# The first expert mixture's outputs: stored in slot order and gathered by token, in place of scattered to token order

## The chip, the core and the metric

The kernel runs on one core of a Trainium2 chip. Five engines work side by side, each on its own queue of instructions in a fixed order: TensorE (PE; its weight loads are listed as PEld), VectorE (DVE), ScalarE (ACT), GpSimd (POOL) and SyncE (SP). They wait for each other through semaphores, and every transfer between the chip's memory and the core's own memory (SBUF) is issued by one of the queues and moved by 16 shared DMA engines. The metric is the device time of one execution in microseconds (us); the median over the runs is compared.

## The reference

The input is 8 sequences of 256 tokens with 256 channels. It goes through three sublayers, each on a layer-normalised copy and added back:

```
x = x + 0.5 * ffn(layernorm(x))
x = x + attn(layernorm(x))
x = x + 0.5 * ffn(layernorm(x))
```

`ffn` is a mixture of 8 experts. Each of the 2048 tokens takes the two experts with the highest gate value; each expert computes `(silu(x @ w_gate) * (x @ w_up)) @ w_down` with a hidden width of 176. The two results are weighted by their gate probabilities and added to a shared feed-forward part of hidden width 352. `attn` has 16 heads of width 128 with one key and one value head; an index score picks the 32 best earlier keys of every query, and the softmax runs over those.

## The kernel before, in words

The 2048 tokens are 16 tiles of 128 (NT = 16), and `x` stays in SBUF all the time. The three sublayers follow one another: `ffn(0, ...)`, the attention, `ffn(1, ...)`. The order on every engine is fixed when the program is built; the building framework moves independent instructions past each other, so that work of one stage can stand among the next one's.

In `ffn`, `layernorm` normalises the tiles and also stores them to `xn_dram` in the chip's memory (line 249). `route` works out, for each token and each of its two choices, a slot: the slots of one expert are consecutive and start at a multiple of 128, so that the slots fall into blocks of 128 rows with one expert each. 37 blocks always run (ND), two more only when they are needed (`rare`, NB = 39). From the slots `route` derives, for each row of each block, the token to fetch (`token`) and the row to write (`dest`).

For block b, `fetch` (L488) has POOL gather 128 rows of `xn_dram` by `token` with an indirect DMA. PE transposes them (`turn`, `px`, L499), multiplies them by the expert's gate and up weights (`widen`, `pgu`, L511), transposes the hidden values (`turn_hidden`, `ph`, L539) and multiplies by the down weights (`narrow`, `py`, L547). ACT makes `sl` (L521) and copies `py` to `y` (L555), DVE makes `h` and `hT` (L523, L541). Then POOL scatters the block's rows with a second indirect DMA (L557) to `y_dram`, each row to the place of its token and choice. Fetches run up to six blocks ahead (XB = 6), and there are four `y` buffers. SP meanwhile loads attention weights, one load per block (L118). The shared part of some tiles (`shared`, L451, L470, L477, L480) is left for after the blocks.

`combine` (L597) brings the expert results of one token tile back. For the first mixture it is called in the attention's `begin`, before the layer norm of the tile:

```python
parts = y_dram[NT * P : (K + 1) * NT * P, :].rearrange("(k i p) d -> i p k d", k=K, p=P)
yg = pool.tile([P, K, D], F32, tag="yg", name=f"yg_{n}_{i}", bufs=bufs)
nc.sync.dma_start(out=yg, in_=parts[i])
```

So it is one plain load of 256 KB by SP (L599), and then two DVE instructions on `x` (L601), weighted with `wt`. There are three `yg` buffers here. In the built order all 16 loads stand on SP right behind the last weight load, and the 32 DVE instructions stand between the shared parts, the layer norms and the first index scores of the attention.

The attention's first steps are `select_keys(0)` and four times `index_queries` and `add_heads`: PE makes `pqi` (L637) and `pi` (L698), ACT copies `qi` (L644) and makes `r` (L706), DVE adds to `index` (L711, L713). POOL zeroes the first 32 columns of each `qi` buffer before (L632). Later POOL scales the softmax weights (L779) and stores them by plain DMAs of its own (L790).

Of the kernel before, what the change touches and what calls it, by code (L numbers as in the profile page):

```python
# [8 lines left out]
F32 = mybir.dt.float32  # L9
BF16 = mybir.dt.bfloat16  # L10
I32 = mybir.dt.int32
# [4 lines left out]
P = 128  # L16
# [7 lines left out]
def macaron_kernel(  # L24
# [19 lines left out]
    nc = tc.nc  # L44

    B, S, D = x_in.shape
    NT = B * S // P
# [8 lines left out]
    K = 2  # L56
# [5 lines left out]
    NB = (NT * P * K) // P + E - 1  # L62
    ND = (NT * P * K) // P + E // 2 + 1
# [14 lines left out]
    small = ctx.enter_context(tc.tile_pool(name="small", bufs=3))  # L78
    psum = ctx.enter_context(tc.tile_pool(name="psum", bufs=2, space=bass.MemoryType.PSUM))
    dram = ctx.enter_context(tc.tile_pool(name="dram", bufs=1, space=bass.MemoryType.DRAM))  # L80


    x = res.tile([P, NT, D], F32, name="x")
# [16 lines left out]
    for g in groups:  # L100
# [6 lines left out]
        out=wsd_sb[:, 0:nfull, :],  # L107
        in_=sw_down[0 : nfull * P, :].rearrange("(c p) d -> p c d", p=P),
# [40 lines left out]
    for h0 in range(0, H, HL):  # L149
        for k in range(KD):  # L150
            cols = slice(h0 * HD, (h0 + HL) * HD)
# [8 lines left out]
    for t, val in ((cap, 3e38), (cbias, 0.0)):  # L160
        nc.gpsimd.memset(t, val)
        nc.gpsimd.affine_select(
            out=t,
            in_=t,
# [10 lines left out]
        out=before,  # L175
        in_=before,
# [9 lines left out]
    def counted(name, pattern, base=0, channel=0, dtype=F32, pool=const):  # L186
        t = pool.tile([P] + [n for _, n in pattern], dtype, name=name, bufs=1)
        nc.gpsimd.iota(
            t, pattern, base=base, channel_multiplier=channel,
            allow_small_or_imprecise_dtypes=True,  # L190
        )
        return t
# [62 lines left out]
    def route(n, lg, place, block, pool, keep, meanwhile):  # L255
# [5 lines left out]
        def t(name, shape, dtype=F32):  # L261
            return pool.tile([P] + shape, dtype, tag=f"r_{name}", name=f"{name}_{n}", bufs=1)
# [60 lines left out]
        )  # L323
        slot = t("slot", [NT, K])
        nc.vector.tensor_reduce(slot, hot, AX.X, ALU.add)
        slot_i = t("slot_i", [NT, K], I32)
        nc.vector.tensor_copy(slot_i, slot)

        meanwhile(3)
# [15 lines left out]
        parts = t("parts", [2, NB, NT * K], BF16)  # L345
# [31 lines left out]
        dest = keep.tile([P, NB], I32, name=f"dest_{n}", bufs=1)  # L377
        nc.vector.tensor_copy(dest, goes)
        token = keep.tile([P, NB], I32, name=f"token_{n}", bufs=1)
# [16 lines left out]
        cols = keep.tile([P, NB], I32, name=f"cols_{n}", bufs=1)  # L396
# [8 lines left out]
        wt = small.tile([P, NT, K], F32, tag="wt", name=f"wt_{n}", bufs=1)  # L405
# [7 lines left out]
        )  # L413
        used = keep.tile([P, 1], I32, name=f"used_{n}", bufs=1)
        nc.vector.tensor_copy(used[0:1], end[0:1, E - 1 : E])
        return wt, token, dest, cols, used

    def ffn(n, pool, block_pool, behind, store):

        xn_dram = dram.tile([NT * P, D], F32, name=f"xn_dram_{n}")
        y_dram = dram.tile([((K + 1) * NT + NB) * P, D], F32, name=f"y_dram_{n}")
        lg = pool.tile([P, NT, E], F32, tag="lg", name=f"lg_{n}", bufs=1)
        sg = {}
        for tiles in groups:
# [116 lines left out]
        def narrow(b):  # L543

            py = psum.tile([P, D], F32, tag="D", name=f"py_{n}_{b}")
            for c in range(2):
                nc.tensor.matmul(  # L547
                    py,
                    hT[b][:, c, :],
                    w[0:HH, bass.ds(c0[b] + 2 * KD * HE + c * D, D)],  # L550
                    start=(c == 0),
                    stop=(c == 1),
                )
            y = block_pool.tile([P, D], F32, tag="y", name=f"y_{n}_{b}", bufs=4)
            nc.scalar.copy(y, py)  # L555

            stored = nc.gpsimd.indirect_dma_start(  # L557
                out=y_dram,
                out_offset=bass.IndirectOffsetOnAxis(ap=dest[:, b : b + 1], axis=0),
                in_=y,  # L560
                in_offset=None,
            ).ins
            tc.declare_no_dep(stored, group=f"y_{n}", reason="rows that differ")
            tc.add_to_no_dep_group(f"y_{n}", stored)

        def routed():


            for b in range(XB):
                fetch(b)  # L570
            locate(0)
            turn(0)
            turn(1)
            for b in range(ND):
                h = widen(b)
                if b > 0:
                    narrow(b - 1)
                if b + XB < ND:
                    fetch(b + XB)
                if b + 2 < ND:  # L580
                    turn(b + 2)
                turn_hidden(b, h)
            narrow(ND - 1)

        def rare(count):

            with tc.If(count > ND):
                for b in range(ND, NB):
                    fetch(b)
                    locate(b)  # L590
                    turn(b)
                    turn_hidden(b, widen(b))
                    narrow(b)

        parts = y_dram[NT * P : (K + 1) * NT * P, :].rearrange("(k i p) d -> i p k d", k=K, p=P)

        def combine(i, pool, bufs):  # L597
            yg = pool.tile([P, K, D], F32, tag="yg", name=f"yg_{n}_{i}", bufs=bufs)
            nc.sync.dma_start(out=yg, in_=parts[i])  # L599
            for k in range(K):  # L600
                nc.vector.scalar_tensor_tensor(  # L601
                    x[:, i, :], yg[:, k, :], wt[:, i, k : k + 1], x[:, i, :], ALU.mult, ALU.add
                )
            if store:
                nc.sync.dma_start(out=outr[:, i, :], in_=x[:, i, :])  # L605

        tiles = iter(range(NT))
# [1 line left out]
        def meanwhile(count):  # L609
            for _ in range(count):  # L610
                shared(next(tiles))

        with tc.tile_pool(name=f"route{n}", bufs=1, reuse_waits="tile") as tables:
            place = counted(f"place_{n}", [[1, P], [0, NA * K]], dtype=BF16, pool=tables)
            block = counted(f"block_{n}", [[1, NB], [0, NT * K]], dtype=BF16, pool=tables)
            wt, token, dest, cols, used = route(n, lg, place, block, tables, pool, meanwhile)
        meanwhile(behind)
        count = nc.values_load(used[0:1, 0:1], min_val=0, max_val=NB)
        routed()
# [222 lines left out]
    with (  # L842
        tc.tile_pool(name="blocks0", bufs=3) as block_pool,
        tc.tile_pool(name="ffn0", bufs=3) as pool,
    ):
        combine = ffn(0, pool, block_pool, behind=2, store=False)

    with tc.tile_pool(name="attn", bufs=3, reuse_waits="tile") as pool:
        wo_sb = pool.tile([P, H, D], F32, tag="wo", name="wo_sb", bufs=1)
# [54 lines left out]
    with (  # L904
        tc.tile_pool(name="blocks1", bufs=3, reuse_waits="tile") as block_pool,
        tc.tile_pool(name="ffn1", bufs=3, reuse_waits="tile") as pool,
    ):
        combine = ffn(1, pool, block_pool, behind=2, store=True)
        with tc.tile_pool(name="late", bufs=1, reuse_waits="tile") as late:
            for i in range(NT):  # L910
                combine(i, late, 8)
# [48 lines left out]
```

## Time and profile before

| | |
|---|---|
| Median of 10 runs | 1011.74 us (1007.07 to 1016.94) |
| Profiled execution | 1009.46 us, of which 1007.7 us are the span of the profile |
| PE busy | 951.6 us, 94% of the span |
| DVE, ACT, POOL busy | 562.1 us (56%), 412.7 us (41%), 290.7 us (29%) |
| POOL's gathers L488, both mixtures | 74 of 967 ns |
| POOL's scatters L557, both mixtures | 74 of 974 ns |
| Loads `yg<-y_dram` L599, both mixtures | 32 of 256 KB |

In the profile, busy time of an engine is the time in which it executed; the timeline gives each instruction's start and duration and, in brackets, how long the engine had been idle before it and what ended that. "issue" means that the profile shows nothing that it waited for. The stretches by the timeline: the blocks of the first mixture run from 68 to 182 us, the attention begins to mix in at 184 us, and the blocks of the second mixture run from 865 to 976 us.

### The profile page before, as it was taken

To read this page: it belongs to the slowest core of one execution; us is meant where nothing else is said; L and a number is where in the kernel's file an instruction comes from. 1 tells how busy PE (TensorE), PEld (TensorE's weight loads), DVE (VectorE), ACT (ScalarE), POOL (GpSimd) and SP (SyncE) were. 2 spreads that over 40 slices of the span, in tenths; PEclk is the share of its full clock that TensorE was granted. 3 is DMA by queue.
4 is the path that set the end of the run, shared out by engine and by line. 5 is a ranking of instruction groups with operands and counts; after the bars stand their busy time and mean duration, and the time that the engine had idled before them with its cause. 6 is when DMAs were issued, how large, how long until landed. Compare 5 with 4: busy or idle time off the path is not lost. (4 is left out here: it accounts for less than half of the span.)

```text
span 1007.7 us, 15179 instructions
## 1 busy us (share of the span) xinstructions
PE 951.6 (94%) x4476; PEld 749.4 (74%) x4476; DVE 562.1 (56%) x1574; ACT 412.7 (41%) x1225; POOL 290.7 (29%) x333
## 2 busy tenths in 40 slices
PE   6989899999999999999999999999989899888896
PEld 4666666698888887888888888888868667666663
DVE  5442222697775676676575675666675636222226
ACT  4423333244635444544444544444444443233321
POOL 2035664100222212212212212222123310566630
PEclk9999999999999999999999999999999999999998
DMA  9314532340332222222222222222223420222227
GB/s 298 85 52 138 172 122 72 112 137 24 105 99 87 73 96 85 77 97 84 74 95 95 87 92 84 88 80 92 87 73 126 142 84 1 73 91 86 91 79 222
DMA packets 99751, 99.65 MB, mean 99 GB/s; under 512 B 12022, under 2 KB 86742, under 8 KB 99670
## 3 DMA queue, kind: packets, MB, share of 16 engines
q1 hardware_dynamic: 82678, 51.63, 17.6%
q0 software_dynamic: 14272, 44.58, 12.5%
q10 hardware_dynamic: 2720, 2.47, 0.8%
q8 instruction: 39, 0.64, 0.3%
q14 instruction: 42, 0.34, 0.1%
HBM read 57.47 MB, written 41.16 MB: 98 GB/s over the span
## 5 line engine op out<-in xcount | busy, mean ns | idle before, releaser
L779 POOL TENSOR_TENSOR s<-s,rden 128x512 f32<-128x512 f32 x64 | 93.7, 1464 | 284.9 <-DVE rden L778 121.4
L769 ACT ACTIVATE s<-s,anm 128x128 f32<-128x128 f32 (+1 forms) x256 | 113.1, 443 | 90.3 <-DVE anm L766 55.6
L833 PEld LDWEIGHTS pwo<-wo_sb,oT 128*128 128x128 f32 x512 | 97.1, 190 | 27.0 <-issue 14.4
L637 PE MATMUL pqT<-xnT,wq_sb 128*128 128x256 f32 x512 | 115.9, 379 | 0.0
L833 PE MATMUL pwo<-wo_sb,oT 128*128 128x256 f32 x512 | 115.8, 379 | 0.0
L488 POOL DMA_INDIRECT xs<-xn_dram,token x74 | 71.6, 967 | 153.1 <-DVE dest L384 56.1
L637 PEld LDWEIGHTS pqT<-xnT,wq_sb 128*128 128x128 f32 x512 | 97.1, 190 | 12.8 <-issue 1.2
L713 DVE SCALAR_TENSOR_TENSOR index<-r,v,index 128x128 f32<-128x128 f32 (+1 forms) x240 | 102.3, 456 | 5.5 <-ACT r L706 4.0
L637 PE MATMUL pqi<-xnT,wi_sb 128*128 128x224 f32 x512 | 102.9, 353 | 0.0
L786 DVE STREAM_TRANSPOSE sq<-s 128x512 f32<-128x512 f32 x64 | 62.5, 977 | 71.2 <-POOL s L779 71.2
L511 PE MATMUL pgu<-wall,xsT 128*128 x296 | 100.8, 462 | 0.0
L750 PE MATMUL ps<-kT,qT 128*128 128x256 f32 (+1 forms) x512 | 95.3, 329 | 3.6 <-DVE s L757 3.6
L637 PEld LDWEIGHTS pqi<-xnT,wi_sb 128*128 128x128 f32 x512 | 95.9, 190 | 2.5 <-issue 1.4
L805 PE MATMUL pav<-s,v 128*128 128x512 f32 x192 | 94.6, 600 | 1.2 <-DMA s<-sq_dram 1.2
L698 PE MATMUL pi<-kT,qi 128*128 128x256 f32 (+1 forms) x512 | 94.0, 334 | 0.4 <-ACT kT L673 0.3
L750 PEld LDWEIGHTS ps<-kT,qT 128*128 128x128 f32 x512 | 80.4, 191 | 18.0 <-issue 3.8
L706 ACT ACTIVATE r<-pi 128x512 f32<-128x512 f32 x96 | 55.9, 594 | 81.9 <-DVE index L713 55.3
L547 PE MATMUL py<-wall,hT 88*128 x296 | 78.6, 388 | 9.8 <-issue 7.4
L698 PEld LDWEIGHTS pi<-kT,qi 128*128 128x128 f32 x512 | 73.3, 191 | 19.4 <-ACT r L706 8.0
L557 POOL DMA_INDIRECT y_dram<-y,dest x74 | 72.1, 974 | 44.8 <-ACT xsT L501 15.9
L547 PEld LDWEIGHTS py<-wall,hT 88*128 88x128 f32 x296 | 55.2, 191 | 35.5 <-issue 13.9
L757 DVE TENSOR_TENSOR s<-ps,mb 128x512 f32<-128x512 f32 x96 | 64.2, 682 | 23.0 <-DMA s<-sq_dram 12.8
(151 smaller groups left out, 1278.0 us busy)
## 6 DMA issues: line engine op xcount, KB each, us to landing
s<-sq_dram SPq DMA_DIRECT2D x384, 64.0 KB
sq_dram<-sq POOLq DMA_DIRECT2D x32, 512.0 KB
yg<-y_dram SPq DMA_DIRECT2D x32, 256.0 KB
sq_dram<-sq POOLq DMA_DIRECT2D x32, 256.0 KB
xn_dram<-xn SPq DMA_DIRECT2D x32, 128.0 KB
wi_sb<-in_L_attn_wq_idx_dram SPq DMA_DIRECT2D x8, 256.0 KB
wq_sb<-in_L_attn_wq_dram SPq DMA_DIRECT2D x8, 256.0 KB
wo_sb<-in_L_attn_wo_dram ACTq DMA_DIRECT2D x8, 256.0 KB
```

The lines of the kernel that those rows point to most:

```text
L488: nc.gpsimd.indirect_dma_start(out=xs[b], out_offset=None, in_=xn_dram, in_offset=bass.IndirectOffsetOnAxis(ap=token[:, b : b + 1], axis=0),)
L511: nc.tensor.matmul(pgu, xsT[b][:, k, :], w[:, bass.ds(c0[b] + 2 * k * HE, 2 * HE)], start=(k == 0), stop=(k == KD - 1),)
L547: nc.tensor.matmul(py, hT[b][:, c, :], w[0:HH, bass.ds(c0[b] + 2 * KD * HE + c * D, D)], start=(c == 0), stop=(c == 1),)
L557: stored = nc.gpsimd.indirect_dma_start(out=y_dram, out_offset=bass.IndirectOffsetOnAxis(ap=dest[:, b : b + 1], axis=0), in_=y, in_offset= ...
L637: nc.tensor.matmul(ps[:, j, :], weights(k, h0 + hh + j), xnT[:, k, b * S + skip : (b + 1) * S], start=(k == 0), stop=(k == KD - 1),)
L698: nc.tensor.matmul(pl[:, j, :], qi[:, hh + j, t * P : (t + 1) * P], kT[:, 1, 0:ns], start=True, stop=True,)
L713: nc.vector.scalar_tensor_tensor(index[t], r[:, j, :], iw, index[t], ALU.mult, ALU.add)
L750: nc.tensor.matmul(ps[:, j, :], qT[:, j0 + j, t * P : (t + 1) * P], kT[:, 0, 0:ns], start=True, stop=True,)
L769: nc.scalar.activation(s[:, j, :], s[:, j, :], AF.Exp, bias=nm[:, j : j + 1], scale=SCALE, accum_out=den[:, j : j + 1],)
L779: nc.gpsimd.tensor_tensor(s, s, rden.unsqueeze(2).to_broadcast([P, HG, ns]), ALU.mult)
L805: nc.tensor.matmul(po.rearrange("p q h k -> p (q h k)"), v[:, c, 0:HD], pT[:, c].rearrange("p q r -> p (q r)"), start=(c == 0), stop=(c == t),
L833: nc.tensor.matmul(po, oT[:, h, :], wo_sb[:, w0 + h, :], start=(h == 0), stop=(h == HW - 1),)
```

## The change

In the first mixture the rows of a block are stored as they are, to the slots of `y_dram` (a plain DMA by SP, 128 rows of 1 KB). `y_dram` is then as long as the slots, and at the start of the kernel its last two blocks, which need not run, are filled with two tiles of `x`. `combine` of the first mixture gathers, on POOL, the row of each token's slot, once per choice, so with two indirect DMAs per tile; `slot_i` is kept for that. The second mixture is as before.

```diff
@@ route
-        slot_i = t("slot_i", [NT, K], I32)
+        slot_i = small.tile([P, NT, K], I32, tag="slot_i", name=f"slot_i_{n}", bufs=1)
...
-        return wt, token, dest, cols, used
+        return wt, slot_i, token, dest, cols, used
@@ ffn
-        y_dram = dram.tile([((K + 1) * NT + NB) * P, D], F32, name=f"y_dram_{n}")
+        rows = ((K + 1) * NT + NB if last else NB) * P
+        y_dram = dram.tile([rows, D], F32, name=f"y_dram_{n}")
+        if not last:
+            nc.sync.dma_start(
+                out=y_dram[ND * P :, :].rearrange("(b p) d -> p b d", p=P), in_=x[:, 0 : NB - ND, :]
+            )
@@ narrow
             nc.scalar.copy(y, py)
+            if not last:
+                nc.sync.dma_start(out=y_dram[b * P : (b + 1) * P, :], in_=y)
+                return
             stored = nc.gpsimd.indirect_dma_start(
                 out=y_dram,
                 out_offset=bass.IndirectOffsetOnAxis(ap=dest[:, b : b + 1], axis=0),
...
@@ combine
-            nc.sync.dma_start(out=yg, in_=parts[i])
+            if last:
+                parts = y_dram[NT * P : (K + 1) * NT * P, :]
+                nc.sync.dma_start(
+                    out=yg, in_=parts.rearrange("(k i p) d -> i p k d", k=K, p=P)[i]
+                )
+            else:
+                for k in range(K):
+                    nc.gpsimd.indirect_dma_start(
+                        out=yg[:, k, :],
+                        out_offset=None,
+                        in_=y_dram,
+                        in_offset=bass.IndirectOffsetOnAxis(ap=slot[:, i, k : k + 1], axis=0),
+                    )
```

In the built order of the changed kernel, SP has the store of `y` of each block among the weight loads; POOL has 39 gathers of `xs` without scatters between them, and then the 32 gathers of `yg`. The zeroing of `qi` (L632 of the kernel before) stands among these: two of them behind the 21st gather, one behind the 30th and one behind the 32nd.

More of the change, by code (lines that the diff above doesn't have):

```diff
@@ L415, in route, with ffn @@
         nc.vector.tensor_copy(used[0:1], end[0:1, E - 1 : E])
-        return wt, token, dest, cols, used
-    def ffn(n, pool, block_pool, behind, store):
+        return wt, slot_i, token, dest, cols, used
+    def ffn(n, pool, block_pool, behind, last):
         xn_dram = dram.tile([NT * P, D], F32, name=f"xn_dram_{n}")
-        y_dram = dram.tile([((K + 1) * NT + NB) * P, D], F32, name=f"y_dram_{n}")
+        rows = ((K + 1) * NT + NB if last else NB) * P
[4 more added lines that the diff above has]
+            )
         lg = pool.tile([P, NT, E], F32, tag="lg", name=f"lg_{n}", bufs=1)
@@ L593, in rare @@
                     narrow(b)
-        parts = y_dram[NT * P : (K + 1) * NT * P, :].rearrange("(k i p) d -> i p k d", k=K, p=P)
         def combine(i, pool, bufs):
             yg = pool.tile([P, K, D], F32, tag="yg", name=f"yg_{n}_{i}", bufs=bufs)
-            nc.sync.dma_start(out=yg, in_=parts[i])
+            if last:
[11 more added lines that the diff above has]
+                    )
             for k in range(K):
@@ L603, in combine @@
                 )
-            if store:
+            if last:
                 nc.sync.dma_start(out=outr[:, i, :], in_=x[:, i, :])
@@ L615, in ffn @@
             block = counted(f"block_{n}", [[1, NB], [0, NT * K]], dtype=BF16, pool=tables)
-            wt, token, dest, cols, used = route(n, lg, place, block, tables, pool, meanwhile)
+            wt, slot, token, dest, cols, used = route(n, lg, place, block, tables, pool, meanwhile)
         meanwhile(behind)
@@ L845, in macaron_kernel @@
     ):
-        combine = ffn(0, pool, block_pool, behind=2, store=False)
+        combine = ffn(0, pool, block_pool, behind=2, last=False)
     with tc.tile_pool(name="attn", bufs=3, reuse_waits="tile") as pool:
@@ L907, in macaron_kernel @@
     ):
-        combine = ffn(1, pool, block_pool, behind=2, store=True)
+        combine = ffn(1, pool, block_pool, behind=2, last=True)
         with tc.tile_pool(name="late", bufs=1, reuse_waits="tile") as late:
```

## Prediction

> **What bounds the kernel now.** I read the page's busy times and slices first: they name the engine that sets the time.
>
> ```profile
> PE 951.6 (94%) x4476; PEld 749.4 (74%) x4476; DVE 562.1 (56%) x1574; ACT 412.7 (41%) x1225; POOL 290.7 (29%) x333
> PE   6989899999999999999999999999989899888896
> POOL 2035664100222212212212212222123310566630
> ```
>
> PE is the bound: 1007.7 - 951.6 = 56 us of the span are idle on it. POOL is dense only in slices 3 to 7 and 35 to 39, the blocks of the two mixtures, and there PE falls to 8. Next I asked for the stretches around the change, by engine (columns: stretch, then busy us of PE, PEld, DVE, ACT and POOL, granted clock, DMA share, GB/s).
>
> ```profile
> 82.00:162.00 80.00, 70.85 (x329) 51.42 (x328) 20.47 (x54) 25.62 (x81) 52.61 (x54) 1.00 0.47 145
> 162.00:184.00 22.00, 20.10 (x91) 14.41 (x92) 6.25 (x16) 7.66 (x24) 8.68 (x10) 1.00 0.16 56
> 184.00:200.00 16.00, 16.00 (x71) 11.27 (x70) 13.82 (x57) 2.66 (x10) 0.30 (x2) 1.00 0.50 148
> 200.00:212.00 12.00, 11.70 (x68) 10.22 (x67) 11.80 (x65) 4.55 (x11) 0.00 (x0) 1.00 0.47 129
> ```
>
> While the blocks run (82 to 162), 9 us of PE are idle. Where the results are combined (184 to 212), PE has no idle time, DVE is busy 25.6 of 28 us, and POOL does nothing. The change takes work from POOL in the first stretch and gives it work in the second. The timeline of PE shows how the idle time of the blocks looks: `px` is one row per block.
>
> ```profile
> 98.36 0.38 PE L499 MATMUL px<-ident,xs 128*128 128x128 f32 x2
> 100.85 0.38 PE L499 MATMUL px<-ident,xs 128*128 128x128 f32 x2
> 103.34 0.38 PE L499 MATMUL px<-ident,xs 128*128 128x128 f32 x2
> 104.99 0.42 PE L539 MATMUL ph<-ident,h 128*88 128x128 f32 x2 [1.26 <-issue]
> 107.30 0.38 PE L499 MATMUL px<-ident,xs 128*128 128x128 f32 x2
> ...
> 163.78 0.38 PE L499 MATMUL px<-ident,xs 128*128 128x128 f32 x2
> 166.27 0.38 PE L499 MATMUL px<-ident,xs 128*128 128x128 f32 x2
> 168.76 0.38 PE L499 MATMUL px<-ident,xs 128*128 128x128 f32 x2
> ```
>
> Two or three blocks follow at 2.49 us, then one takes 3.96; from 163.78 on none is late. POOL's timeline has the same rhythm.
>
> ```profile
> 97.11 0.97 POOL L488 DMA_INDIRECT xs<-xn_dram,token  x1 [1.51 <-PE pgu L511]
> 98.38 0.98 POOL L557 DMA_INDIRECT y_dram<-y,dest  x1 [0.30 <-issue]
> ...
> 103.49 0.98 POOL L557 DMA_INDIRECT y_dram<-y,dest  x1 [0.30 <-issue]
> 105.97 0.97 POOL L488 DMA_INDIRECT xs<-xn_dram,token  x1 [1.50 <-PE ph L539]
> ...
> 167.12 0.96 POOL L557 DMA_INDIRECT y_dram<-y,dest  x1 [1.53 <-ACT xsT L501]
> 169.60 0.96 POOL L557 DMA_INDIRECT y_dram<-y,dest  x1 [1.53 <-ACT xsT L501]
> ```
>
> A gather and a scatter take 0.97 + 0.98 + 2 x 0.30 = 2.55 us, slightly more than PE's 2.49: POOL issues without a pause, and after every six indirect DMAs both POOL and PE stop for over a microsecond. Once the gathers are issued (from 160 us) POOL has one DMA per block, it pauses 1.5 us before each, and PE, which does the same work per block until 174, has no stop. The stops are also in the second mixture, where SP loads no weights, and not in the attention, where SP issues many more transfers. So I read them as a price of back-to-back indirect DMAs on POOL, whose mechanism the profile doesn't name.
>
> **Part 1, the scatters leave POOL: a gain of 12.6 us.** From the `px` at 81.48 (block 4) to the one at 173.74 (block 36) the timeline takes 92.26 us for 32 blocks. At 2.49 each they take 79.7, 12.6 less. After the change POOL has 0.97 + 0.30 = 1.27 us of work in 2.49, as it had from 162 on, so I take all of it. Bounds: 0, if the gathers alone cause the stops (no stretch shows sparse gathers without scatters), and 12.6. I take the upper end, since the nearest stretch, one DMA per block, has no stop. The first stop (PE waits 3.74 us at 76.64, behind ten back-to-back gathers) stays.
>
> **Part 2, the stores on SP: nothing.** There are 37 plain DMAs. A weight load's issue on SP takes 0.37 us, so a load and a store are 0.74 of 2.49 us per block. The store waits for ACT's `y`; behind it on SP are the attention's weight loads, first needed at 203 us (L678), 70 us after the last is issued (133). That cover would have to shrink by tens of us to cost anything. A `y` buffer comes back after four blocks, 10 us; the scatter at 181.54 and the load that waits for it at 184.21 show that such a store lands in under 2.7.
>
> **Part 3, the fill of the last two blocks: 0.9 us lost.** It is one 256 KB store on SP, ahead of the `xn` stores and expert loads, and it waits only for `x`'s first tiles, for which these wait too. In the first 25 us the DMA engines are full at 299 GB/s; 256 KB there are 0.9 us. DVE waits 9.25 us at 34.3 for an `xn` store in that queue, and PE 1.15 us for DVE. I count it whole; if PE finds other work it is 0.
>
> **Part 4, the 32 gathers of `yg`: 4.5 us lost, and 2 more.** They replace 16 loads on SP. The last `y` is copied at 181.27; with 2.7 us to land, POOL's first gather is issued at 184.0, as SP's first load was (184.21). Two gathers are 2 x (0.97 + 0.30) = 2.54 us. With 2.6 us from issue to landing (the load issued at 184.21 is used at 186.95), tile i is complete at 187.9 + 2.54 i. DVE's second L601 of tile 5 started at 196.91, of tile 11 at 210.66, of tile 15 at 223.38: they become 3.7, 5.2 and 2.6 us late. DVE has no idle time to make this up, so it is about 5.2 us late when the index scores begin. PE's slack is small there: ACT ends the copy of `qi` at 226.71 and PE's `pi` begins at 226.88, and in the first group 214.50 and 215.28, so 0.2 to 0.8 us. That leaves about 4.5 us on PE. Behind the gathers on POOL wait the zeroings of `qi`: the first two behind 21 gathers, at 184.0 + 21 x 1.27 = 210.7, while PE wants them at 209.5 plus the delay that it already has, so they are hidden as long as the delay is over 1.2 us. 32 gathers back to back can also bring the stops of part 1 with them: at one in six, five of 1.3 us, 6.5 us if none falls into time that PE waits anyway, 0 if all do. I take 2, since PE already waits for part of that time.
>
> One more cost has no row of its own: what a gather does to DVE's instructions beside it. In the blocks DVE reads one operand from PSUM; an L601 reads two from SBUF. The nearest rows are these, from the timelines of POOL and DVE in the attention.
>
> ```profile
> 256.29 1.89 POOL L779 TENSOR_TENSOR s<-s,rden 128x1024 f32<-128x1024 f32 x1 [1.58 <-DVE rden L778]
> 259.98 0.59 POOL L790 DMA_DIRECT2D sq_dram<-sq  x1 [1.80 <-DVE sq L786]
> ```
>
> ```profile
> 256.72 1.75 DVE L713 SCALAR_TENSOR_TENSOR index<-r,v,index 128x256 f32<-128x256 f32 x1
> 259.62 0.44 DVE L713 SCALAR_TENSOR_TENSOR index<-r,v,index 128x256 f32<-128x256 f32 x1
> ```
>
> Beside POOL's arithmetic the same DVE instruction takes 1.75 us in place of 0.44; beside POOL's plain DMA it takes 0.44. A gather is a DMA, but one that reads a list of slots. Bounds: 0 by the second pair, 32 x 0.97 = 31 us by the first. I take 0, as a DMA issue is the nearer row.
>
> [...]
>
> **The sum.** -12.6 + 0.9 + 4.5 + 2.0 = -5.2 us. The profiled execution took 1009.46 us (span 1007.7), so 1004.3 there. The median of the runs is 2.28 us above that execution; 1011.74 - 5.2 = 1006.5.
>
> **Rivals.**
> - *The stops belong to gathers, not to density.* For it: the first stop follows ten gathers with no scatter among them. Against it: those ten were back to back. No gain then, 0.9 + 4.5 + 2 to 6.5 lost: 1019 to 1024.
> - *Slower: the gather blocks DVE.* Place: 184 to 225 us, where DVE is full. Price: up to 0.97 us per gather, 31 us, and with the rest of the sum 1011.74 - 5.2 + 31 = 1037. It decides from 5.2 / 32 = 0.16 us per gather upwards. For it speaks the row of 1.75 us, against it the row of 0.44.
> - *The two ends cancel.* The stops go, but in the combining stretch all five come back on PE's path and the gathers run a little slower: 6.5 for 2, and 0.1 us per gather, 3.2, give -5.2 + 4.5 + 3.2 = +2.5: 1009 to 1014.
> - That the change doesn't do what it says: excluded, as the built order has the 37 stores on SP and no scatter on POOL in the first mixture.
>
> **How the numbers follow.** Forecast 0.46, around its own range of 1000 (the gain less the fill alone: 1011.74 - 11.7) to 1008.7; cancelling 0.14; stops that stay 0.22; blocked DVE 0.18. A measurement can tell about 0.3% from no change, 3.0 us, so faster means under 1008.7 and slower over 1014.8: 0.46, 0.14, 0.40. The range starts at 1000 and ends at 1024, the upper end of the stops that stay, which also takes in a DVE blocked by up to about half a microsecond per gather; what is left out is the rest of that rival.
>
> **What would show it.** Right: `px` rows 2.49 us apart from 81 to 174 in the changed profile, and the first L601 rows of tile 11 some 5 us later, measured from the last `y` copy. Part 1 is wrong if stops of 1.2 us still stand every few blocks; part 4 is wrong if L601 rows take over 0.5 us, or if gathers of `yg` take over 1 us or stand much further apart than 1.27; part 3 if DVE's wait at 34 us doesn't grow. If the second mixture's time changes, something is at work that I haven't listed.

## The result, and the profile after

The changed kernel takes 1019.45 us (median of 18 runs, 1016.93 to 1023.72) beside 1010.97 for the kernel before: a ratio of 1.0085, 95% interval 1.007 to 1.010. It is slower by 8.5 us where the prediction had it faster by 5.2. The profiled execution took 1019.36 us, its span is 1017.5.

The page of the changed kernel: busy times, POOL's slices and the granted clock of TensorE.

```profile
PE 957.9 (94%) x4476; PEld 756.1 (74%) x4476; DVE 563.9 (55%) x1574; ACT 412.8 (41%) x1225; POOL 285.9 (28%) x328
POOL 2032331550322221222122222212213310566630
PEclk9998999689999999999999999999999999999998
```

PE does the same 4476 matmuls and is busy 6.3 us longer. The third line shows a lower clock in three slices where before had 9: an 8 in slice 4, behind the first stop, and a 6 and an 8 in slices 8 and 9, just where POOL now has 5 and 5, its gathers of `yg`. The stretches of the prediction, in the changed kernel:

```profile
82.00:162.00 80.00, 80.00 (x386) 61.39 (x386) 24.27 (x64) 30.90 (x97) 25.50 (x27) 1.00 0.49 151
162.00:184.00 22.00, 17.50 (x73) 11.53 (x71) 9.32 (x25) 3.96 (x14) 8.66 (x10) 0.94 0.24 73
184.00:200.00 16.00, 11.91 (x30) 7.79 (x29) 7.25 (x34) 1.25 (x6) 8.35 (x9) 0.61 0.28 82
212.00:230.00 18.00, 13.28 (x60) 11.19 (x59) 12.23 (x58) 5.38 (x10) 7.19 (x9) 0.81 0.43 117
```

In the blocks PE has no idle time left (80.00 of 80 us, 70.85 before): part 1 of the prediction, in full. Behind the blocks PE is idle for 4.5, 4.1 and 4.7 us of the last three stretches, and the granted clock is 0.61 and 0.81 in the last two, where it was 1.00. The timeline of PE shows both:

```profile
99.16 0.38 PE L506 MATMUL px<-ident,xs 128*128 128x128 f32 x2
101.65 0.38 PE L506 MATMUL px<-ident,xs 128*128 128x128 f32 x2
...
182.66 0.90 PE L477 MATMUL ptg<-ident,gt 128*128 128x128 f32 x3 [3.41 <-issue]
191.51 0.84 PE L477 MATMUL ptg<-ident,gt 128*128 128x128 f32 x3 [1.92 <-issue]
195.69 2.93 PE L484 MATMUL po<-wsd_sb,gT 128*128 128x256 f32 x6 [2.16 <-ACT gT L478]
...
217.27 2.08 PE L718 MATMUL pi<-kT,qi 128*128 128x128 f32 x6 [4.55 <-issue]
```

The `px` rows of the blocks are 2.49 us apart from 84 us on, all 31 times. Then come four waits of 1.9 to 4.6 us. Behind them three `ptg` take 0.90 us, which take 0.49 at full clock: PE goes on at half speed (granted clock 0.50 from 182.6 to 186 us). If every matmul's start is laid beside that of the same matmul in the trace of before, PE is 12.3 us early at the end of the blocks and 9.5 us late from the matmul that started at 212.6 us in before (222.1 in the changed kernel); that is 21.8 us lost in 45. From there on the difference stays between 9.3 and 9.8 us for all but a dozen of the matmuls, through the second mixture too.

What ends the waits is of two kinds. DVE's timeline shows the first:

```profile
181.69 0.48 DVE L621 SCALAR_TENSOR_TENSOR x<-yg,wt,x 128x256 f32<-128x256 f32 x1 [0.19 <-issue]
182.09 0.51 DVE L466 TENSOR_TENSOR gt<-sg,pu 128x352 f32<-128x352 f32 x1
```

The `gt` that PE waits for until 182.66 has its matmul done by 177.8, but stands in DVE's queue behind five L621 of tiles 0 to 2, which wait for one gather after the other. ACT's timeline shows the second kind ("remote": the profile can't name what ended the wait), and POOL's has gathers back to back, here those beside the second of ACT's rows:

```profile
195.26 0.37 ACT L478 COPY gT<-ptg 128x256 f32<-128x256 f32 x1 [11.08 <-remote]
216.69 0.53 ACT L664 COPY qi<-pqi 128x448 f32<-128x448 f32 x1 [5.23 <-remote]
```

```profile
214.71 0.94 POOL L614 DMA_INDIRECT yg<-y_dram,slot_i  x1 [0.30 <-issue]
215.95 0.94 POOL L614 DMA_INDIRECT yg<-y_dram,slot_i  x1 [0.30 <-issue]
```

PE finished the `ptg` that the first copy waits for at 192.35 (the row at 191.51 plus 0.84), and the `pqi` of the second at 211.57. ACT starts 2.9 and 5.1 us later, though nothing else kept it busy; a row of sixteen gathers had just ended at 192.30 in the first case. These look like the stops that the prediction read in the blocks of before, now longer.

### The profile page after: what moved, and what is told of

Read it like the earlier page. It is cut to its first block, busy times and chain, and to the rows that moved or that the text cites. A ratio compares the mean times of both kernels' runs of the same rounds, so it can differ in the third digit from the quotient of the medians.

```text
span 1017.5 us, 15217 instructions
## 1 busy us (share of the span) xinstructions
PE 957.9 (94%) x4476; PEld 756.1 (74%) x4476; DVE 563.9 (55%) x1574; ACT 412.8 (41%) x1225; POOL 285.9 (28%) x328
## 5 line engine op out<-in xcount | busy, mean ns | idle before, releaser
L718 PE MATMUL pi<-kT,qi 128*128 128x256 f32 (+1 forms) x512 | 96.1, 339 | 5.1 <-issue 4.6
L777 DVE TENSOR_TENSOR s<-ps,mb 128x512 f32<-128x512 f32 x96 | 64.2, 682 | 21.8 <-PE ps L770 19.0
L530 DVE TENSOR_TENSOR h<-sl,pgu 128x176 f32<-128x176 f32 x74 | 25.0, 337 | 83.3 <-ACT sl L528 74.0
```

What stands on the lines that cost most here:

```text
L718: nc.tensor.matmul(pl[:, j, :], qi[:, hh + j, t * P : (t + 1) * P], kT[:, 1, 0:ns], start=True, stop=True,)
L777: nc.vector.tensor_tensor(s[:, j0 : j0 + nh, :], ps, bias[t].unsqueeze(1).to_broadcast([P, nh, ns]), ALU.add,)
```

## The experiments

Two causes stand for the loss: the **pace** (theory P: DVE gets a tile's rows every 2.5 us and passes its wait on to PE) and the **stops** (theory S: what PE signals arrives late while POOL issues indirect DMAs back to back). Theory C has the stops belong to the chip and not to the instructions; one more, called G or the third theory below, is that a gather costs something by itself, wherever it stands. The runs went to five chips, and their numbers matter: the kernel before takes 977 us on four of them and 1011 on chip 7, as in the first runs. Each ratio is to the kernel before on the same chip; a single run has none.

| run | chip | median us | before | ratio (95% interval) |
|---|---|---|---|---|
| before_again | 3 | 976.36 (one run) | 976.99 | |
| after_again | 3 | 983.68 | 976.99 | 1.0069 (1.0055 to 1.0083) |
| spread_loads | 3 | 975.29 | 976.99 | 0.9983 (0.9969 to 0.9996) |
| held_apart | 3 | 998.07 | 976.99 | 1.0213 (1.0198 to 1.0227) |
| plain_loads | 13 | 991.09 | 977.21 | 1.0145 (1.0129 to 1.016) |
| idle_gathers | 13 | 975.99 | 977.21 | 0.999 (0.9981 to 0.9999) |
| late | 13 | 978.82 | 977.21 | 1.0016 (1.0006 to 1.0025) |
| held_late | 13 | 1016.98 | 977.21 | 1.041 (1.0391 to 1.0429) |
| chained_loads | 7 | 1000.74 | 1011.06 | 0.9907 (0.9886 to 0.9929) |
| late_apart | 7 | 1010.08 | 1011.06 | 0.9993 (0.9968 to 1.0017) |
| idle_gathers_again | 7 | 1018.64 (one run) | 1011.06 | |
| paced | 15 | 1004.22 | 976.61 | 1.0278 (1.0259 to 1.0297) |
| late_apart_again | 15 | 978.27 | 976.61 | 1.0016 (1.0007 to 1.0025) |
| trickled | 0 | 1010.38 | 977.31 | 1.0344 (1.0328 to 1.036) |

### Both kernels again, on another chip

No edit.

> The kernel before, unchanged, for its profile beside those of the same chip. On the chip of the first four runs it took 977 us, 34 less than in the runs that the prediction was made from, and the run with idle gathers, which is the same kernel in the blocks, had px rows 2.49 us apart without a single stop, with a gather and a scatter back to back all the time. Theory C (the stops belong to the chip or its state, not to the instructions): here either no stop in the first mixture, the second and behind the routing, and 974 to 980 us, or, on a chip with stops, all of them and 1005 to 1017. Theory S (density of indirect DMAs): stops as in the first profile, 1005 to 1017.

> The changed kernel, unchanged, beside the kernel before on this chip. If there are no stops here, part 1 has nothing to remove, and what is left is the price of the gathers: theory P (pace) expects the wait of PE for DVE in the shared parts, 3.4 us and some 2 to 5 us of half clock behind it, and late index scores, in all 5 to 12 us slower, ratio 1.005 to 1.012. Theory S expects long stops of 2 to 5 us in the stretch of the gathers here too, 15 to 22 us slower. If there are stops as in the first profiles, ratio 1.007 to 1.010 again.

The window over the blocks of before_again:

```profile
82.00:162.00 80.00, 79.99 (x383) 60.68 (x382) 24.31 (x65) 30.43 (x94) 56.05 (x58) 1.00 0.47 149
```

POOL is busier than in the first profile (56.05 against 52.61 us), with the same gather and scatter back to back, and PE has no idle time: no stop. So density alone does not make the stops; the chip has a part in them, as theory C says, and part 1 has nothing to remove here. What the gathers cost without stops is in after_again: 6.7 us. Its PE timeline, then DVE's, which shows the cause of the first wait:

```profile
175.57 0.55 PE L477 MATMUL ptg<-ident,gt 128*128 128x128 f32 x3 [3.00 <-DVE gt L466]
203.25 2.65 PE L718 MATMUL pi<-kT,qi 128*128 128x128 f32 x12 [1.93 <-ACT qi L664]
```

```profile
173.29 0.48 DVE L621 SCALAR_TENSOR_TENSOR x<-yg,wt,x 128x256 f32<-128x256 f32 x1 [0.61 <-DMA yg<-y_dram,slot_i]
174.60 0.48 DVE L621 SCALAR_TENSOR_TENSOR x<-yg,wt,x 128x256 f32<-128x256 f32 x1 [0.16 <-DMA yg<-y_dram,slot_i]
175.00 0.51 DVE L466 TENSOR_TENSOR gt<-sg,pu 128x352 f32<-128x352 f32 x1
```

Against before_again PE is 0.95 us early before these waits, 3.96 late behind the first and 7.62 behind the second: the waits are 3.00 and 1.93, the rest is mainly the clock (0.86 from 172 to 184 us, 0.91 from 200 to 220). It is at half for 3.4 us each time; behind the second wait (columns: stretch, busy us of PE, granted clock, DMA share, GB/s):

```profile
204.40:207.80 3.40, 3.40 (x12) 0.51 0.62 216
```

So waits of 1.93 and 3.00 us here, and of 3.41 us on the first chip, each had half clock behind them; waits of 0.95 to 1.12 us in the run late left it at 1.00 (granted clock from 160 to 240 us).

### The gain without the gathers

```diff
-                for k in range(K):
-                    nc.gpsimd.indirect_dma_start(out=yg[:, k, :], in_=y_dram, ...)
+                nc.sync.dma_start(out=yg, in_=y_dram[...])   # plain_loads: rows 256 i to 256 i + 255
+                                                             # spread_loads: two rows of each 32, from block 5 on
```

> The changed kernel with the gathers of the first mixture replaced by 16 plain loads of SP, 256 KB each, of consecutive rows of the stored results (the gather by token is left out). The theories agree here. The changed kernel reached the end of the blocks 12.2 us before the kernel before and lost 21 us behind them, in the stretch of the gathers. If the whole loss is in the gathers, this kernel keeps the 12.2: 997 to 1001 us against 1011, ratio 0.986 to 0.990, px rows 2.49 us apart, no wait of PE over 1 us between 170 and 215 us and a granted clock of 1.00 there. If the stores of y by SP or the fill have a share in the loss, it stays over 1002.

> The changed kernel with the 32 gathers replaced by 16 plain loads of SP of the same size (the gather by token is left out). Each load takes rows from all of blocks 5 to 36, so that none can go out before the last block is stored; in the run with loads of consecutive rows these went out between the blocks, and DVE waited there for them. No gather, no pace: on a chip without stops, within 2 us of the kernel before (0.998 to 1.003: the fill and the stores alone); on a chip with stops 10 to 13 us faster.

plain_loads missed: the first rows are stored early, so the loads and the combining moved into the blocks, where DVE waited for them (one row of its timeline) and PE for DVE's `hT`; the kernel is 14 us slower than the one before.

```profile
87.85 1.01 DVE L618 SCALAR_TENSOR_TENSOR x<-yg,wt,x 128x256 f32<-128x256 f32 x2 [1.20 <-DMA yg<-y_dram]
```

spread_loads, whose loads can't go out before the last block, is at 0.9983: the fill and the stores on SP cost nothing that shows, and the 6.7 us on this chip come with the gathers.

### Gathers that nobody waits for

```diff
+            if n == 0 and i < 8:      # in the kernel before, on POOL, each behind the first load of yg
+                for k in range(K):
+                    nc.gpsimd.indirect_dma_start(out=idle, in_=xn_dram, ...)   # idle is not read
```

> The kernel before, with 16 more indirect DMAs on POOL behind the first load of yg, one after the other, into a small tile that nobody reads. Theory S (signals): while POOL issues indirect DMAs without a pause, what PE signals to ACT and DVE arrives late, from about the tenth one on. Then PE, which waits for nothing that these gathers bring, stops one to three times for 1 to 4 us between 195 and 212 us, its granted clock falls to about 0.5 behind each stop, and the kernel is 3 to 10 us slower: 1014 to 1021, ratio 1.003 to 1.010. Theory P (pace): only the late arrival of yg makes DVE and then PE late. Then nothing happens here: 1010 to 1012, ratio 0.999 to 1.001, no stop.

> The run with 16 idle gathers once more, in case these runs go to another chip: if the blocks of the second mixture show the stops of the first profiles here, the idle gathers show whether PE stops beside them too, without waiting for any of them (theory S: one to three stops of 1 to 4 us between 170 and 200). On a chip without stops, as before: no stop, 974 to 978 us.

Each of the 16 gathers fetches 128 pieces of 256 bytes, a quarter of a token. The same kernel ran on two chips. On chip 13 PE's timeline has two waits between 160 and 215 us, both also in before_again: 1.07 us at 164.37 at the end of the blocks, and this one.

```profile
183.32 1.56 PE L477 MATMUL po<-wsd_sb,gT 128*128 128x256 f32 x6 [0.30 <-ACT gT L471]
```

On chip 7, with a row of POOL's timeline beside:

```profile
203.47 2.93 PE L477 MATMUL po<-wsd_sb,gT 128*128 128x256 f32 x6 [5.35 <-issue]
209.93 1.86 PE L477 MATMUL po<-wsd_sb,gT 128*128 128x256 f32 x6 [2.45 <-ACT gT L471]
```

```profile
202.23 0.94 POOL L606 DMA_INDIRECT idle<-xn_dram,token  x1 [0.30 <-issue]
```

Nothing that PE needs comes from these gathers. On chip 13 they cost nothing, on chip 7 PE stops for 5.35 and 2.45 us beside them and goes on at half clock (2.93 for 1.56 us); the one run takes 1018.64 us where the highest of before is 1014.04. So theories S and C were each half right: in these runs the stops stood beside back-to-back indirect DMAs, and only on a chip that has them.

### The pace

```diff
             for i in tiles:
-                combine(i, small, 3)
+                with tc.issue_after(combine.up[(12, 12, 14, 15)[min(i, 3)]].ins):   # late: behind the gt of that tile
+                    combine(i, small, 3)
```

In late_apart tiles 8 to 15 stand behind `scored[HG * ((i - 8) // 2)]`, a last index addition. chained_loads is spread_loads with a dependency of each load on the one before it.

> The changed kernel with the same gathers, but the combining instructions of DVE stand later in its queue: those of tiles 0 and 1 behind gt of tile 12, of tile 2 behind gt of tile 14, all others behind gt of tile 15, so that no gt waits behind a yg that has not arrived. Theory P (pace): PE's waits of 3.41 us at 182.66 and of about 2 us at 191.51 and 195.69 go, and with them the half clock; left are some 3 to 5 us of late index scores: 1000 to 1005, ratio 0.989 to 0.994. Theory S (signals): 32 gathers still go out without a pause, only the first wait goes (3.4 us and its 2.6 us of half clock), stops of 1 to 5 us stay: 1008 to 1016, ratio 0.997 to 1.005.

> The run with spread loads, in which each of the 16 loads of SP waits until the one before it has landed (again the gather by token is left out, and POOL issues nothing in this stretch). A load takes some 2.7 us from issue to use, so a tile arrives every 2.5 to 3 us, as with two gathers of 1.25 us each, where the free loads come about 2 us apart and ahead of need. Theory P (it is the pace at which yg arrives, whoever brings it): slower than the kernel before like the changed kernel, by 4 to 14 us, ratio 1.004 to 1.014, with a wait of PE for gt in the shared parts or for qi in the index scores and a granted clock of 0.5 behind it. Theory G (it is something that the gathers on POOL do to the other engines): as the spread loads, 0.997 to 1.000.

> The run late, with the combining instructions of tiles 8 to 15 also moved in DVE's queue: those of tiles 8 and 9 behind the last index addition of the first four heads, of 10 and 11 behind that of the next four, and so on, so that no index addition waits behind a gather under way. Theory P: the last wait (1.12 us for qi and the half clock behind it, 1.9 us in all) goes, and the kernel is within 1 us of the spread loads: 0.997 to 1.000 on a chip without stops, 0.985 to 0.992 on one with the stops of the first profiles, where the 12 us of part 1 would be kept. Theory G: 1.001 or more.

> The run late_apart beside it, on the same chip, with the 32 gathers back to back. On a chip with stops 0.997 to 1.002, as before, with waits of PE of 1.1 to 3.2 us between 180 and 210; on a chip without stops 0.997 to 1.000 with none over 1 us, if only the pace made the run late slower there (1.0016).

Without stops, the order in DVE's queue alone takes the changed kernel from 1.0069 to 1.0016: the wait of 3.00 us is gone. The stretch in which it stood, in before_again, after_again and late:

```profile
172.00:184.00 12.00, 11.70 (x54) 8.49 (x54) 11.76 (x56) 2.46 (x10) 0.00 (x0) 1.00 0.42 120
172.00:184.00 12.00, 9.00 (x32) 5.93 (x31) 9.97 (x44) 1.06 (x4) 9.22 (x10) 0.86 0.37 109
172.00:184.00 12.00, 11.70 (x54) 8.49 (x53) 11.42 (x42) 2.40 (x9) 8.21 (x10) 1.00 0.31 91
```

The other 0.16% stayed, in late and in late_apart_again; moving tiles 8 to 15 took the wait for `qi` away and brought nothing more in the ratio, against the expectation. PE's timeline in late_apart_again has one wait left that before_again doesn't have, 0.95 us for `xn` at 191.65; the rest of the 1.6 us is not settled.

On chip 7 chained_loads keeps the gain: its blocks have no stop behind the first one, and 10.3 us are left.

```profile
84.00:152.00 68.00, 68.00 (x330) 52.24 (x329) 20.81 (x55) 26.46 (x82) 24.93 (x28) 1.00 0.56 168
```

Behind the blocks it loses 2.0 us (PE waits 1.09 us for `qi` at 204.82), less than the 4 to 14 expected, since in its built order the `gt` stood ahead of the late tiles. It is a weak witness for the pace; late against after_again is the strong one. late_apart on that chip has the gathers and little of the pace; its PE timeline:

```profile
181.84 1.56 PE L484 MATMUL po<-wsd_sb,gT 128*128 128x256 f32 x6 [1.35 <-issue]
...
206.08 2.93 PE L719 MATMUL pi<-kT,qi 128*128 128x128 f32 x8 [3.17 <-issue]
```

Its blocks run as fast as those of chained_loads: PE is 12.0 us early against the trace of before. Between 178 and 220 us it loses 11 of them. The same kernel without stops, late_apart_again, loses 2 us there, so some 9 go to such stops and the half clock behind them. So, on a chip with stops, most of the 12 us that the scatters gave back go to the gathers.

### A better place for the gathers

The edits, in the attention's loop (held_late; held_apart holds the gathers there too and puts the combining four heads later), in `combine` (paced) and behind `weigh` (trickled):

```diff
-                begin(b + 2 + g0 // (2 * HG), b + 3 + g0 // (2 * HG))
+                with tc.issue_after(latest[0].ins):     # POOL's last scaling or zeroing
+                    begin(b + 2 + g0 // (2 * HG), b + 3 + g0 // (2 * HG))
```

```diff
+                    if len(chain) > 2 * K:              # paced: from the fifth gather on
+                        tc.add_manual_dep(chain[-1].ins, chain[-2].ins.name, ...)
```

```diff
                 pT = weigh(b, t, g0, qT, kT, bias, pool)
+                trickle()                               # one gather behind the store, a tile one store later
```

> As the run late for tiles 0 to 3; the gathers of the other twelve tiles are held back on POOL and go out in the attention, four at a time, behind a scaling of softmax weights. So only 8 gathers go out without a pause, fewer than the ten before which no stop was seen. Theory S and theory P both expect the gain of the blocks to stay: 998 to 1003, ratio 0.987 to 0.992, no wait of PE over 1 us between 172 and 215. A third theory, that a gather costs PE something wherever it stands, expects the loss to move into the attention: 1008 to 1018.

> As the run held_late in which the gathers of tiles 4 to 15 go out in the attention, with two differences: the combining instructions of these tiles stand four heads later in DVE's queue than their gathers in POOL's, so that DVE does not wait for a gather that has just been issued; and the first four tiles are as in the changed kernel. In held_late PE waited 4 us and more several times between 224 and 600 us for DVE and ACT, 37 us in all. If that was DVE waiting in its queue for gathers that stood behind POOL's scaling, it goes, and what is left on a chip without stops is the wait in the shared parts: ratio 1.002 to 1.010. If gathers cost the attention something else, it stays above 1.02.

> As the run late_apart, but from the fifth gather on each waits until the one before it has landed, so POOL issues one gather per 2.5 to 2.7 us, as it does in the blocks of the changed kernel, in place of one per 1.25; DVE's combining instructions are moved further back to fit (tiles 4 and 5 behind the first four heads' index additions, the last ones in the first softmax). The same 32 gathers with the same rows. On a chip with stops, theory S (density) expects no stop over 1 us between 172 and 250 and the 12 us of part 1 kept: 998 to 1002, ratio 0.987 to 0.992, where late_apart took 0.9993; if a gather costs a stop whatever its distance, it stays at 0.997 or more. On a chip without stops both expect 0.997 to 1.002.

> The changed kernel with its gathers spread out as the work allows. Tiles 0 and 1 as in the run late. The four gathers of tiles 2 and 3 go out one after the other's landing, and are combined behind the first four heads' index additions. The other 24 go out in the attention, one behind each store of softmax weights (L810), where POOL is idle over half of the time, and each tile is combined one store later, so that DVE never waits for a gather. In held_apart four gathers in a row stood between a scaling and its store, and each such group made PE about 3.5 us late; one gather at a time is 1.25 us on an engine that then waits. Theory P and S together: nothing waits for a gather and none are dense. On a chip without stops 0.996 to 1.002; on a chip with stops the 12 us of part 1 stay: 0.985 to 0.991. If a gather in the attention costs PE its own 1.25 us on the path, 24 of them make 1.02 to 1.03.

All four are 2 to 4% slower than the kernel before, far from what was expected, on chips without stops. In paced a gather follows the one before it after 2.9 us or more, mostly 2.9 to 3.8, its issue and its landing, not 2.6 (a row of POOL's timeline), and DVE, whose combining was placed for 2.6, waits again, 16.1 us in all. In held_late DVE waits 14.2 us for gathers.

```profile
176.18 0.94 POOL L617 DMA_INDIRECT yg<-y_dram,slot_i  x1 [2.09 <-DMA yg<-y_dram,slot_i]
```

In trickled DVE doesn't wait for gathers, but PE does for DVE: the layer norms now stand in the attention, and PE's transposes of `xn` stand in PE's fixed order ahead of other work.

```profile
355.58 0.69 PE L252 MATMUL pt<-ident,xn 128*128 128x128 f32 x2 [4.28 <-DVE xn L245]
```

So these four don't show that a gather costs something wherever it stands. They point to the combining and the layer norm behind it, which are cheap early and dear late; no run moved these alone. Whether paced gathers make no stop on chip 7 is open: none of these four went there. No version of the changed kernel that gathers `yg` beats the kernel before beyond its interval, on either kind of chip.

## Why the prediction was wrong

- **Part 1** was right on its own chip: 12.3 us for 12.6, `px` rows 2.49 us apart, and the first stop (72 to 82 us) stayed. One gather per 2.49 us makes no stop there. What it didn't know is that the stops belong to the chip as well: on chips 3 and 13 the blocks of before have none and the term is 0, and on chips 15 and 0 the kernel before takes 977 us too.
- **Part 2** was right; **part 3** was 0.9 us too high: DVE's wait grew from 9.25 to 9.66 us, as foretold, and the routing began 0.55 us later (41.45 for 40.90), but the first gather of `xs` went out no later (62.90 for 63.21), and spread_loads has no loss.
- **Part 4** had the mechanism and the wrong place. It looked for DVE's lateness at tile 11, where the index scores begin, and found little slack there. (It took DVE to have no idle time; its own rows leave 2.4 of 28 us.) But L621 of tiles 0 to 2 already stand ahead of a `gt` that PE waits for. Without stops the term measured 8.6 us on chip 3 (from 0.95 early to 7.62 late) for the predicted 4.5. The half clock behind a long wait, 1.6 to 1.7 us each time on chip 3 and 2.6 to 2.7 behind the first and the last wait on the recorded chip, was in no term, though the trace of before had it behind the stop of 3.74, a clock of 0.53 and 0.50:

```profile
76.60:78.00 1.40, 1.36 (x4) 1.10 (x5) 0.73 (x2) 0.00 (x0) 0.56 (x1) 0.53 0.14 43
78.00:80.00 2.00, 2.00 (x6) 1.37 (x6) 0.00 (x0) 0.00 (x0) 0.00 (x0) 0.50 0.39 101
```

- **The step that decided** is "I take 2": the stops beside the gathers. It took five stops of 1.3 us, bounds 0 and 6.5. On the recorded chip PE's signals come up to 5.1 us late, with half clock behind the waits: 21.8 us less the 8.6 of pace leaves about 13, and late_apart shows some 9 with little pace. The nearer rows for 32 gathers in a row were the two stops of before behind nine gathers with nothing between them (the prediction counted ten): the one of 3.74 us that it named, and one in the second mixture:

```profile
872.24 0.42 PE L539 MATMUL ph<-ident,h 128*88 128x128 f32 x2 [1.58 <-DVE h L523]
```

Three of these are 5 to 16 us, an estimate from 1.58 us and from 3.74 plus 1.7 of half clock, so 6.5 was no upper bound. By the starts of the matmuls the terms came out as 12.3 us gained for 12.6, nothing for 0.9, and 21.8 lost for 6.5.
- **Rivals.** The blocked DVE is refuted: its L621 take 473 ns beside the gathers (32 rows, 165 to 240 us) and 477 over both mixtures, as their L601 took before (476). The pair of rows that the prediction went by couldn't show it, since the DVE row at 259.62 ends 0.08 us after POOL's DMA began. "Stops that stay" gave 1019 to 1024 and holds the time, but by the wrong way: the stops of the blocks went. "The two ends cancel" named the way, stops that come back in the combining stretch, and priced it too low by the same bound.

The row of the L621:

```profile
L621 DVE SCALAR_TENSOR_TENSOR x<-yg,wt,x 128x256 f32<-128x256 f32 x64 | 29.7, 477 | 11.3 <-DMA yg<-y_dram 6.6 <-DMA yg<-y_dram,slot_i 4.0 <-issue 0.4
```

The second mixture didn't change, as foretold: PE is 9.5 us late where it begins and 9.8 near its end.

## What to carry to other kernels

When a change makes data arrive later, look in the consumer's queue for what stands behind the first instruction that waits, and not only for who needs the data; a wait of PE of 1.9 us and more cost some 1.6 to 2.7 us on top in half clock here. Price a burst by the bursts that the trace has, not by a mean over a mixed stretch. And before a rhythm in one trace is read as a law, see whether another chip shows it: here the whole expected gain was such a rhythm.

## What was not expected of the hardware

The same kernel takes 977 us on four chips and 1011 on another, at a granted clock of 1.00 in the blocks of both (82 to 162 us, before and before_again). The 34 us lie in the blocks of the two mixtures, 18 and 16, where one trace has stops and the other none. Why only some chips have them is open, but there is a trail: in the trace of the changed kernel on the first chip, of the 16 landing records of a gather of `yg`, at most six are there while gathers go out back to back, and 12 or all 16 only beside a pause; on chip 3 all 16 are there every time. The whole trace holds 13805 semaphore records on the first chip and 15477 on chip 3, for the same 15217 instructions. In the stretch of the gathers, 172 to 222 us, it holds 255 where chip 3 has 648 for the same work; in the attention behind it, 9599 and 9674. So it is in all the traces: the five with stops (the two first profiles and the three of chip 7) hold 13372 to 14015 such records, the eleven without 15222 to 15487. Records are missing from the first gather of `yg` on, before any stop beside them. So stops and missing records go together here; whether one brings the other, or something else brings both, is not shown: every timed run was recorded too, and a run without recording wasn't tried.
